# Layer 0's scores and values as 64×64 matmuls on the quadrants of the array, in turns

## The chip, the cores and the metric

The kernel runs on one core of one Trainium2 chip. A core has TensorE (PE, with its weight loads shown as PEld), VectorE (DVE), ScalarE (ACT), GpSimd (POOL) and SyncE (SP, which here issues DMAs), all with instruction queues of their own that meet through semaphores. The metric is the device time of the whole program in microseconds (us). Before the change it is 2517.85 us, the median of three runs (2517.65 to 2518.61). The profiled execution is a separate one; its span is 2627.8 us, and all times inside it are read against that span.

## The reference

Two layers work on 8 items of 1024 tokens with 256 channels. The change touches only the attention of layer 0:

```
qkv = (xt @ w_qkv + b_qkv).reshape(B, S, 8, 3 * 64)
q, k, v = jnp.split(qkv, 3, axis=-1)
attn = jnp.einsum('bihd,bjhd->bijh', q, k) * SCALE
attn = jax.nn.softmax(attn, axis=1)
res = jnp.einsum('bijh,bjhd->bihd', attn, v).reshape(B, S, 512)
res = res @ w_out + b_out + xt
```

The softmax runs over axis 1, the queries i: for one key j the exponentials over all queries are summed. So the sum belongs to a key, and the kernel divides the values of a key by it instead of the weights. Layer 1 is a single-head attention with a layer norm, then a mixture of 8 experts with 2 chosen per token. All is in f32.

## The kernel before

The items are worked one after the other: layer 0 of an item (`layer0`), its layer 1 attention (`attend`), norm and routing. The routing of an item (`gates`, `dispatch`) is a generator whose small pieces are put into the steps of the next item's layer 0. The experts follow after seven items; the eighth has its experts computed densely.

In `layer0` the 8 heads form 4 pairs g (`NPAIR`). Heads of a pair lie on partitions 0 to 63 and 64 to 127 of the q and k tiles. There are 32 steps `at`, that is 4 pairs times 8 blocks j of 128 keys. One step works one key block of both heads h:

- `score(at, h, n)` is a matmul of 64 rows (the head's channels), 128 columns (the keys) and 512 queries (half n). It writes one PSUM bank of the tile `psc`, of which the pool `ps_big` has three (two banks each, shared with the projections `pqk` and others). Head 0 uses the upper half of the array's rows, head 1 the lower, so that two of them can run side by side.
- `first_max` (DVE, line 401) takes the maximum over the first 512 queries, and `soften` (DVE, line 413) over the second, giving `nmax`. ACT then writes the exponentials `ex` with their sum (line 423), which frees the `psc` tile. After head 1, DVE takes the reciprocal of the sums (line 430) and scales the values to `vs` (line 432).
- `gather_values(at)` runs two steps later (`LAG = 2`): four matmuls of 128 rows (keys), 64 columns (channels of one head) and 512 queries, which accumulate over the 8 key blocks in the two banks `po`. After the last key block ACT copies both banks to `res` (line 457).
- In steps j = 3 and j = 5 of the first three pairs `project` computes q or k of the next pair: four full-array matmuls `pqk` (line 299), evicted by DVE (line 289).

The loop in `layer0` emits per step: score (at, 0, 0), then score (at-1, 1, 1), scores (at, 0, 1) and (at, 1, 0), then the four value matmuls. DVE's order of the maxima is pinned by `tc.issue_after`. The framework's planner settles each engine's final order and adds the semaphores; in the built program each step has four scores in a row and then four values in a row on PE.

A tile of `psc` is reused by the third allocation after it: score (at+1, 0, 0) takes the tile of (at-1, 1) and so waits for its exponential.

Of the kernel before, what the change touches and what calls it, by code (L numbers as in the profile page):

```python
# [12 lines left out]
AF = mybir.ActivationFunctionType  # L13
ALU = mybir.AluOpType
AX = mybir.AxisListType


@with_exitstack
def kernel(
# [23 lines left out]
    nc = tc.nc  # L43
    P = 128
# [3 lines left out]
    DK = 64  # L48
    SCALE = DK ** (-0.5)
    NCC = C // P  # L50
    NT = S // P
    NH2 = S // 512
# [21 lines left out]
    def big(name):  # L74

        return ps_big.tile([P, 1024], F32, tag="big", name=name)

    def acc(name):

        return ps_acc.tile([P, 512], F32, tag="acc", name=name)  # L80
# [126 lines left out]
    def bcast(t, n):  # L207

        return t.unsqueeze(2).to_broadcast([P, NT, n])
# [159 lines left out]
    def layer0(b, xT, begun, routing):  # L369

        v, qks = begun.v, begun.qks
        array = None
        res = one.tile([P, NPAIR, S], F32, tag="res", name=f"res_{b}")
        steps = [(g, j) for g in range(NPAIR) for j in range(NT)]
        LAG = 2
        seconds = {}  # L380
        pss, firsts, nmaxes, exps, sums, vss = {}, {}, {}, {}, {}, {}
        po = None

        def score(at, h, n):
            g, j = steps[at]
            q, k = qks[g]
            if n == 0:
                pss[at, h] = big(f"psc_{b}_{g}_{j}_{h}")
            r = slice(h * DK, (h + 1) * DK)
            mm = nc.tensor.matmul(  # L390
                pss[at, h][:, ts(n, 512)], k[r, ts(j, P)], q[r, ts(n, 512)], start=True, stop=True
            )
            if n == 1:

                tc.declare_no_dep(mm.ins, firsts.pop((at, h)).ins, reason="the other bank")

        def first_max(at, h):

            g, j = steps[at]
            nmax = small.tile([P, 1], F32, tag="nmax1", name=f"nmax1_{b}_{g}_{j}_{h}")  # L400
            firsts[at, h] = nc.vector.tensor_reduce(  # L401
                nmax, pss[at, h][:, ts(0, 512)], AX.X, ALU.max, negate=True
            )
            nmaxes[at, h] = nmax

        def soften(at, h):

            g, j = steps[at]
            ps = pss.pop((at, h))
            if h == 0:  # L410
                sums[at] = small.tile([P, 2], F32, tag="sums", name=f"sums_{b}_{g}_{j}")
            nmax = small.tile([P, 1], F32, tag="nmax", name=f"nmax_{b}_{g}_{j}_{h}")
            seconds[h] = nc.vector.tensor_scalar(  # L413
                scrap,
                ps[:, ts(1, 512)],
                -1.0,
                nmaxes.pop((at, h)),
                ALU.mult,
                ALU.min,
                accum_out=nmax,  # L420
            )
            ex = expp.tile([P, 1024], F32, tag="exps", name=f"ex_{b}_{g}_{j}_{h}")
            nc.scalar.activation(  # L423
                ex, ps, AF.Exp, bias=nmax, scale=1.0, accum_out=sums[at][:, h : h + 1]
            )
            exps[at, h] = ex
            if h == 1:

                rs = small.tile([P, 2], F32, tag="rs", name=f"rs_{b}_{g}_{j}")
                nc.vector.reciprocal(rs, sums.pop(at))  # L430
                vs = four.tile([P, 2, DK], F32, tag="vs", name=f"vs_{b}_{g}_{j}")
                nc.vector.tensor_mul(
                    vs,
                    v[:, j, ts(g, P)].rearrange("p (h d) -> p h d", d=DK),
                    rs.unsqueeze(2).to_broadcast([P, 2, DK]),
                )
                vss[at] = vs

        def gather_values(at):
            nonlocal po  # L440
            g, j = steps[at]
            if j == 0:
                po = [acc(f"po_{b}_{g}_{n}") for n in range(NH2)]
            vs = vss.pop(at)
            exs = [exps.pop((at, h)) for h in range(2)]
            for n in range(NH2):
                for h in range(2):
                    mm = nc.tensor.matmul(  # L448
                        po[n][h * DK : (h + 1) * DK, :],
                        vs[:, h, :],  # L450
                        exs[h][:, ts(n, 512)],
                        start=(j == 0),
                        stop=(j == NT - 1),
                    )
            if j == NT - 1:
                for n in range(NH2):
                    nc.scalar.copy(res[:, g, ts(n, 512)], po[n])
            return mm

        last = len(steps) - 1  # L460
        for at in range(last + LAG + 1):
            if at <= last:
                score(at, 0, 0)
            if 0 < at <= last + 1:
                score(at - 1, 1, 1)
                soften(at - 1, 1)
            if at <= last:

                with tc.issue_after(seconds[1].ins) if 1 in seconds else nullcontext():
                    first_max(at, 0)  # L470
                score(at, 0, 1)
                score(at, 1, 0)
                soften(at, 0)
                with tc.issue_after(seconds[0].ins):
                    first_max(at, 1)
            if at == 0:
                begun.rest()
                next(routing, None)
            if at >= LAG:
                array = gather_values(at - LAG)  # L480
            if at <= last:
                g, j = steps[at]
                if g + 1 < NPAIR and j in (3, 5):
                    if j == 3:
                        qks.append([])
                    qks[g + 1].append(project(b, xT, g + 1, len(qks[g + 1])))
                if array is not None:
                    with tc.issue_after(firsts[at, 1].ins), tc.issue_after(array.ins):
                        next(routing, None)
        for _ in routing:  # L490
            pass


        t1 = one.tile([P, NT, C], F32, tag="t1", name=f"t1_{b}")
        n = 1024 // C
        for i in range(0, NT, n):
            pt = big(f"pt_x_{b}_{i}")
            for j in range(n):
                for cc in range(NCC):
                    nc.tensor.transpose(  # L500
                        pt[:, j * C + cc * P : j * C + (cc + 1) * P], xT[:, cc, ts(i + j, P)], ident
                    )
            nc.vector.tensor_add(
                t1[:, i : i + n, :],
                pt.rearrange("p (j c) -> p j c", c=C),
                b_o.unsqueeze(1).to_broadcast([P, n, C]),
            )
        for i in range(NT):
            pr = acc(f"pr_{b}_{i}")
            for g in range(NPAIR):  # L510
                nc.tensor.matmul(  # L511
                    pr[:, :C], res[:, g, ts(i, P)], wo[:, g, :], start=(g == 0), stop=(g == NPAIR - 1)
                )
            nc.vector.tensor_add(t1[:, i, :], pr[:, :C], t1[:, i, :])
        return t1


    def attend(b, t1, fill, step=nothing):
# [22 lines left out]
        def scores(i):  # L541
# [10 lines left out]
            nmax = small.tile([P, 1], F32, tag="nmax", name=f"nmax_{b}_{i}")  # L552
            nc.vector.tensor_reduce(nmax, psc, AX.X, ALU.max, negate=True)  # L553
            ex = expp.tile([P, 1024], F32, tag="exps", name=f"ex1_{b}_{i}")
# [55 lines left out]
    def gates(b, lT):  # L610


        def tmp(tag):
            return small.tile([P, NT, E], F32, tag=tag, name=f"{tag}_{b}", bufs=1)

        def col(tag):
            return small.tile([P, NT], F32, tag=tag, name=f"{tag}_{b}", bufs=1)
# [12 lines left out]
        m = col("g_m")  # L630
        nc.vector.tensor_reduce(m, l, AX.X, ALU.max)
        p = tmp("g_p")
# [3 lines left out]
        z = col("g_z")  # L636
        nc.vector.tensor_reduce(z, p, AX.X, ALU.add)
        nc.vector.reciprocal(z, z)
# [3 lines left out]
        def first_of_max(src, tag):  # L642
            top, best = col(f"{tag}_top"), col(f"{tag}_best")
            hot = tmp(f"{tag}_hot")
            nc.vector.tensor_reduce(top, src, AX.X, ALU.max)
            nc.vector.tensor_tensor(hot, src, bcast(top, E), ALU.is_equal)
            yield
            nc.vector.tensor_mul(hot, hot, rank)
            nc.vector.tensor_reduce(best, hot, AX.X, ALU.max)
            nc.vector.tensor_tensor(hot, hot, bcast(best, E), ALU.is_equal)  # L650
# [565 lines left out]
```

## Time and profile before

| | us | share of the span or count |
|---|---|---|
| time, median of 3 | 2517.85 | |
| span of the profiled run | 2627.8 | |
| PE busy | 2504.9 | 95% |
| DVE busy | 1538.1 | 59% |
| ACT busy | 891.0 | 34% |
| POOL busy | 386.0 | 15% |
| layer 0 of one item (559 to 720 us): span 161, PE busy | 151.01 | |
| the same stretch, DVE and ACT busy | 111.04 and 80.41 | |

How to read it: busy PE time is the union of records, whose ends are modelled, so it says that PE is rarely without work and not that the array is full. An f32 matmul appears as two records (passes) and two weight loads, so 1024 score matmuls are x2048. A row of the list of groups has line, engine, operation, written and read tiles, shapes and count, then busy time, mean of one in ns, and the engine's idle time before them with what ended most of it. A row of the timeline has start, length, engine, line, operation and count; neighbouring equal instructions are merged.

### The profile page before, as it was taken

How to read it: one execution, taken by the hardware profiler on the slowest of the kernel's cores; microseconds unless marked ns; L12 is line 12 of the kernel's file. 1: busy time of each engine (PE TensorE's matmuls, PEld its weight loads, DVE VectorE, ACT ScalarE, POOL GpSimd, SP SyncE). 2: the span in 40 equal slices, each digit the busy share in tenths (PEclk: the TensorE clock that was granted, in tenths of full speed). 3: DMA queues.
4: the chain of work that ended last, by engine and by line, in shares of the span. 5: the costliest groups of instructions: out<-in, count | busy, mean ns of one | idle time of the engine just before them, and what ended most of it. 6: DMA issues, size and time to landing. Idle time of an engine off the chain costs nothing.

```text
span 2627.8 us, 27548 instructions
## 1 busy us (share of the span) xinstructions
PE 2504.9 (95%) x9919; PEld 1311.3 (50%) x9919; DVE 1538.1 (59%) x3738; ACT 891.0 (34%) x1491; POOL 386.0 (15%) x383
## 2 busy tenths in 40 slices
PE   9999989998999989998999899989998999997798
PEld 3346434643365336532563256324643488884566
DVE  5764766466656765576557664766476753334443
ACT  3541345134512542244214431444144422221212
POOL 0000020002000100002000200020002144435561
PEclk9999999999999999999999999999999999998899
DMA  7991000000000000000000000000000156663352
GB/s 289 385 333 44 32 33 17 1 17 33 1 17 17 19 15 17 16 1 33 17 17 1 32 17 0 17 32 1 0 17 33 53 196 225 214 196 100 104 166 103
DMA packets 82513, 187.61 MB, mean 71 GB/s; under 512 B 13992, under 2 KB 23880, under 8 KB 80584
## 3 DMA queue, kind: packets, MB, share of 16 engines
q1 hardware_dynamic: 57368, 118.65, 12.6%
q0 software_dynamic: 25008, 67.20, 8.2%
q8 instruction: 78, 1.28, 0.2%
q14 instruction: 59, 0.48, 0.1%
HBM read 100.49 MB, written 110.90 MB: 80 GB/s over the span
## 4 chain that ended last, share of the span: by engine, by line
PE 88%; DVE 3%; another core or an unknown queue 3%; issue 2%; DMA 2%; ACT 2%; SPq 0%; ACTq 0%; POOL 0%; DVEq 0%; POOLq 0%
PE psc L390 19%; PE po L448 17%; PE pqk L299 9%; PE py L571 8%; PE ps L545 7%; PE pr L511 4%; PE pv L335 4%; PE ph L903 3%; PE pe L928 3%; PE pdy L1110 2%; PE pdh L1086 2%; PE px L530 2%; PE pa L564 2%; PE pt_n L232 1%
## 5 line engine op out<-in xcount | busy, mean ns | idle before, releaser
L423 ACT ACTIVATE ex<-psc,nmax 128x1024 f32<-128x1024 f32 x512 | 570.5, 1114 | 639.5 <-DVE scrap L413 576.2
L390 PE MATMUL psc<-qk,qk 64*128 64x512 f32 x2048 | 553.3, 622 | 12.6 <-ACT ex L423 8.1
L413 DVE TENSOR_SCALAR_CACHE_REDUCE scrap<-psc,nmax 128x512 f32<-128x512 f32 x512 | 384.2, 750 | 229.7 <-PE psc L390 137.4
L448 PE MATMUL po<-ex,vs 128*64 128x512 f32 x2048 | 495.9, 605 | 2.1 <-DVE nmax L401 2.1
L390 PEld LDWEIGHTS psc<-qk,qk 64*128 64x128 f32 x2048 | 209.8, 185 | 337.7 <-ACT ex L423 176.1
L401 DVE TENSOR_REDUCE nmax<-psc 128x1 f32<-128x512 f32 x512 | 347.4, 679 | 16.6 <-PE psc L390 16.0
L299 PE MATMUL pqk<-xT,wqkv 128*128 128x512 f32 x512 | 249.8, 633 | 53.8 <-ACT ex L423 53.8
L448 PEld LDWEIGHTS po<-ex,vs 128*64 128x64 f32 x2048 | 124.8, 136 | 337.7 <-issue 212.5
L571 PE MATMUL py<-n,aT 128*128 128x256 f32 x1024 | 244.4, 393 | 16.7 <-DVE aT L566 11.9
L571 PEld LDWEIGHTS py<-n,aT 128*128 128x128 f32 x1024 | 196.0, 195 | 81.9 <-DVE aT L566 49.7
L545 PE MATMUL ps<-nT,xa 128*128 128x512 f32 x512 | 236.5, 592 | 0.0
L692 POOL TENSOR_TENSOR t<-t,n 128x2048 f32<-128x2048 f32 x8 | 36.3, 4537 | 1280.2 <-issue 1004.4
L299 PEld LDWEIGHTS pqk<-xT,wqkv 128*128 128x128 f32 x512 | 99.1, 201 | 195.8 <-issue 102.6
L763 POOL DMA_INDIRECT rows<-n,d_at x112 | 109.2, 975 | 593.3 <-DVE d_at L757 561.3
L556 ACT ACTIVATE ex<-ps,nmax 128x1024 f32<-128x1024 f32 x64 | 71.3, 1115 | 352.2 <-DVE nmax L553 321.9
L576 DVE SCALAR_TENSOR_TENSOR t<-py,rs,t 128x256 f32<-128x256 f32 x64 | 31.0, 484 | 232.6 <-PE py L571 201.7
L289 DVE TENSOR_SCALAR qk<-pqk,b_qk 128x512 f32<-128x512 f32 x100 | 75.1, 751 | 121.4 <-PE pqk L299 121.4
L545 PEld LDWEIGHTS ps<-nT,xa 128*128 128x128 f32 x512 | 93.6, 190 | 79.9 <-issue 73.7
L975 POOL DMA_INDIRECT yk<-y,yat x112 | 112.4, 1003 | 122.1 <-DVE o L1007 71.8
L335 PE MATMUL pv<-wqkv,xT 128*128 128x512 f32 x256 | 119.6, 596 | 1.0 <-ACT wqkv L105 1.0
L553 DVE TENSOR_REDUCE nmax<-ps 128x1 f32<-128x1024 f32 x64 | 78.3, 1224 | 59.1 <-PE ps L545 54.1
L511 PE MATMUL pr<-wo,res 128*128 128x256 f32 x512 | 111.8, 379 | 0.0
(191 smaller groups left out, 2426.9 us busy)
## 6 DMA issues: line engine op xcount, KB each, us to landing
rows<-wb SPq DMA_DIRECT2D x7, 8192.0 KB
y<-yb SPq DMA_DIRECT2D x63, 256.0 KB
xT<-in_x_dram SPq DMA_DIRECT2D x7, 1024.0 KB
sums<-t SPq DMA_DIRECT2D x7, 1024.0 KB
o<-sums SPq DMA_DIRECT2D x7, 1024.0 KB
out_dram<-oT SPq DMA_DIRECT2D x14, 512.0 KB
wpack<-in_L_ffn_w_dram SPq DMA_DIRECT2D x4, 1024.0 KB
wb<-in_L_ffn_w_dram SPq DMA_DIRECT2D x16, 256.0 KB
```

Source lines behind the costliest of these rows:

```text
L299: mm = nc.tensor.matmul(pq[:, ts(n, 512)], wqkv[:, cc, t, ts(g, P)], xT[:, cc, ts(n, 512)], start=(cc == 0), stop=(cc == NCC - 1),)
L335: nc.tensor.matmul(pv, self.xT[:, cc, ts(i, P)], wqkv[:, cc, 2, :], start=(cc == 0), stop=(cc == NCC - 1),)
L390: mm = nc.tensor.matmul(pss[at, h][:, ts(n, 512)], k[r, ts(j, P)], q[r, ts(n, 512)], start=True, stop=True)
L401: firsts[at, h] = nc.vector.tensor_reduce(nmax, pss[at, h][:, ts(0, 512)], AX.X, ALU.max, negate=True)
L413: seconds[h] = nc.vector.tensor_scalar(scrap, ps[:, ts(1, 512)], -1.0, nmaxes.pop((at, h)), ALU.mult, ALU.min, accum_out=nmax,)
L423: nc.scalar.activation(ex, ps, AF.Exp, bias=nmax, scale=1.0, accum_out=sums[at][:, h : h + 1])
L448: mm = nc.tensor.matmul(po[n][h * DK : (h + 1) * DK, :], vs[:, h, :], exs[h][:, ts(n, 512)], start=(j == 0), stop=(j == NT - 1),)
L511: nc.tensor.matmul(pr[:, :C], res[:, g, ts(i, P)], wo[:, g, :], start=(g == 0), stop=(g == NPAIR - 1))
L545: nc.tensor.matmul(psc[:, ts(n, 512)], xa[:, ec, ts(i, P)], nT[:, ec, ts(n, 512)], start=(ec == 0), stop=(ec == NCC - 1),)
L571: nc.tensor.matmul(py[:, :D], aT[:, ts(m, P)], n1[:, m, :], start=(m == 0), stop=(m == NT - 1))
L763: nc.gpsimd.indirect_dma_start(out=view[:, :], out_offset=bass.IndirectOffsetOnAxis(ap=at[:, i : i + 1], axis=0), in_=n2[:, i, :], in_offs ...
L975: nc.gpsimd.indirect_dma_start(out=yk[:, i, k, :], out_offset=None, in_=self.group.y[:, :], in_offset=bass.IndirectOffsetOnAxis(ap=ats[k][ ...
```

## The change

Scores and values are cut into matmuls of 64 rows by 64 columns, so that both kinds use the same quarter tiles of the array and no change of tiling lies between them. A score of 128 keys becomes two of 64 keys (c = 0, 1) into the two partition halves of the same bank. A value matmul over 128 keys becomes two over 64 keys each (`half`), on the upper or lower rows. Both halves must add into the same bank; so they take turns: in turn 0 the upper half works on bank 0 and the lower on bank 1, in turn 1 the reverse. `gather_values` is called twice a step, and the step becomes scores, values, scores, values.

A value group of one half must not write a bank while the other half still does. This is kept by a relay: after each half's last matmul an empty instruction (`nop`) is put on another engine (GpSimd for the first item, SyncE for the others), which waits for PE; the first matmul of the other half in the next turn waits for it.

```diff
+        relay = nc.gpsimd if b == 0 else nc.sync
...
-            mm = nc.tensor.matmul(
-                pss[at, h][:, ts(n, 512)], k[r, ts(j, P)], q[r, ts(n, 512)], start=True, stop=True
-            )
...
+            for c in range(2):
+                mm = nc.tensor.matmul(
+                    pss[at, h][ts(c, DK), ts(n, 512)],
+                    k[r, j * P + c * DK : j * P + (c + 1) * DK],
+                    q[r, ts(n, 512)],
...
-        def gather_values(at):
+        def gather_values(at, turn):
...
+            for half in range(2):
+                keys = ts(half, DK)
+                n = (half + turn) % 2
                 for h in range(2):
                     mm = nc.tensor.matmul(
-                        po[n][h * DK : (h + 1) * DK, :],
-                        vs[:, h, :],
-                        exs[h][:, ts(n, 512)],
-                        start=(j == 0),
-                        stop=(j == NT - 1),
+                        po[n][ts(h, DK), :],
+                        vss[at][keys, h, :],
+                        exps[at, h][keys, ts(n, 512)],
+                        start=(j == 0 and turn == 0),
+                        stop=(j == NT - 1 and turn == 1),
                     )
+                    if h == 0 and (j > 0 or turn > 0):
+                        tc.add_manual_dep(mm.ins, turned[1 - half].ins.name, BEHIND)
+                turned[half] = relay.nop()
+                tc.add_manual_dep(turned[half].ins, mm.ins.name, BEHIND)
...
                 soften(at - 1, 1)
+            if at >= LAG:
+                gather_values(at - LAG, 0)
             if at <= last:
...
             if at >= LAG:
-                array = gather_values(at - LAG)
+                array = gather_values(at - LAG, 1)
```

More of the change, by code (lines that the diff above doesn't have):

```diff
@@ L15 @@
 AX = mybir.AxisListType
+BEHIND = mybir.DependencyInfo(mybir.DependencyClass.Sync, mybir.DependencyReason.DATA)
 @with_exitstack
@@ L379, in layer0 @@
         LAG = 2
-        seconds = {}
+        seconds, turned = {}, {}
+        relay = nc.gpsimd if b == 0 else nc.sync
         pss, firsts, nmaxes, exps, sums, vss = {}, {}, {}, {}, {}, {}
@@ L389, in score @@
             r = slice(h * DK, (h + 1) * DK)
-            mm = nc.tensor.matmul(
-                pss[at, h][:, ts(n, 512)], k[r, ts(j, P)], q[r, ts(n, 512)], start=True, stop=True
-            )
-            if n == 1:
-                tc.declare_no_dep(mm.ins, firsts.pop((at, h)).ins, reason="the other bank")
+            for c in range(2):
[3 more added lines that the diff above has]
+                    q[r, ts(n, 512)],
+                    start=True,
+                    stop=True,
+                )
+                if n == 1:
+                    tc.declare_no_dep(mm.ins, firsts[at, h].ins, reason="the other bank")
         def first_max(at, h):
@@ L437, in soften @@
                 vss[at] = vs
-        def gather_values(at):
+        def gather_values(at, turn):
             nonlocal po
             g, j = steps[at]
-            if j == 0:
+            if j == 0 and turn == 0:
                 po = [acc(f"po_{b}_{g}_{n}") for n in range(NH2)]
-            vs = vss.pop(at)
-            exs = [exps.pop((at, h)) for h in range(2)]
-            for n in range(NH2):
+            for half in range(2):
+                keys = ts(half, DK)
+                n = (half + turn) % 2
                 for h in range(2):
                     mm = nc.tensor.matmul(
-                        po[n][h * DK : (h + 1) * DK, :],
-                        vs[:, h, :],
-                        exs[h][:, ts(n, 512)],
-                        start=(j == 0),
-                        stop=(j == NT - 1),
-                    )
+                        po[n][ts(h, DK), :],
[3 more added lines that the diff above has]
+                        stop=(j == NT - 1 and turn == 1),
+                    )
+                    if h == 0 and (j > 0 or turn > 0):
+                        tc.add_manual_dep(mm.ins, turned[1 - half].ins.name, BEHIND)
+                turned[half] = relay.nop()
+                tc.add_manual_dep(turned[half].ins, mm.ins.name, BEHIND)
+            if turn == 0:
+                return mm
+            vss.pop(at)
+            for h in range(2):
+                exps.pop((at, h))
             if j == NT - 1:
```

## The prediction

> **What bounds the kernel now.** First the shares: PE is busy 95% of the span, and the chain that ended last is 88% PE. So layer 0 has to be read from PE's own timeline. The groups of the lines concerned (busy us, mean ns, then idle time before them):
>
> ```profile
> L423 ACT ACTIVATE ex<-psc,nmax 128x1024 f32<-128x1024 f32 x512 | 570.5, 1114 | 639.5 <-DVE scrap L413 576.2
> L390 PE MATMUL psc<-qk,qk 64*128 64x512 f32 x2048 | 553.3, 622 | 12.6 <-ACT ex L423 8.1
> L413 DVE TENSOR_SCALAR_CACHE_REDUCE scrap<-psc,nmax 128x512 f32<-128x512 f32 x512 | 384.2, 750 | 229.7 <-PE psc L390 137.4
> L448 PE MATMUL po<-ex,vs 128*64 128x512 f32 x2048 | 495.9, 605 | 2.1 <-DVE nmax L401 2.1
> L401 DVE TENSOR_REDUCE nmax<-psc 128x1 f32<-128x512 f32 x512 | 347.4, 679 | 16.6 <-PE psc L390 16.0
> ```
>
> Scores and values hold PE for 1049 us, and waits before them are only 12.6 and 2.1 us. What a pass costs is seen where nothing switches, in layer 1:
>
> ```profile
> 507.61 1.88 PE L545 MATMUL ps<-nT,xa 128*128 128x512 f32 x4
> 509.32 1.04 PE L564 MATMUL pa<-ident,ex 128*128 128x128 f32 x8
> ```
>
> Four passes take 1.71 us from start to start: 0.43 each. In layer 0:
>
> ```profile
> 583.81 3.70 PE L299 MATMUL pqk<-xT,wqkv 128*128 128x512 f32 x8
> 587.44 2.04 PE L390 MATMUL psc<-qk,qk 64*128 64x512 f32 x8
> 589.40 1.94 PE L448 MATMUL po<-ex,vs 128*64 128x512 f32 x8
> 591.27 2.06 PE L390 MATMUL psc<-qk,qk 64*128 64x512 f32 x8
> ```
>
> Eight passes two at a time would be 1.71. The scores take 1.96, the values 1.87, and the projection 3.63 for 3.43. So each change of tiling costs 0.16 to 0.25 us, and a step 3.83, of which 3.42 is streaming.
>
> The other chain in a step leads from a score to the reuse of its `psc` tile:
>
> ```profile
> 670.32 0.75 DVE L413 TENSOR_SCALAR_CACHE_REDUCE scrap<-psc,nmax 128x512 f32<-128x512 f32 x1 [0.73 <-PE psc L390]
> ...
> 671.17 1.11 ACT L423 ACTIVATE ex<-psc,nmax 128x1024 f32<-128x1024 f32 x1 [1.15 <-DVE scrap L413]
> ...
> 672.19 0.19 ACT L423 ACTIVATION_READ_ACCUMULATOR ex<-psc,nmax 128x1 f32 x1
> ```
>
> The first score pair of this block, begun at 669.14, has streamed by 670.10; DVE starts 0.22 later, ACT 0.85 after that, and ACT ends 1.21 later (672.38). A weight load elsewhere (592.21) starts 0.05 after such an end (592.16). Score start to reuse is 0.86 + 0.22 + 0.85 + 1.21 + 0.05 = 3.19 us. Before, score (at-1, 1, 1) opens a step and the tile is wanted when the next opens, 3.83 later: no wait.
>
> **The Trainium skill.** "TensorEngine Tiling (Array Packing)", Tiling Modes: changing the tiling mode, not merely the tile, drains the array. The trace agrees, with 0.16 to 0.25 us. The same page, Restrictions and Gotchas: different row tiles cannot write the same PSUM bank at once; hence the relay. No run shows a breach. "TensorE: Matmul & The Clock Gate", Part 3: matmuls on disjoint tiles run side by side. The trace agrees for two (eight passes in 1.87 us); four at once it doesn't show.
>
> **Part by part.** (1) Count and streaming: score and value instructions double, each on a quarter instead of half of the array. With four at once 16 + 16 passes are again 8 slots of 0.43 = 3.42 us a step. A quarter's weight load has 64 columns, 0.14 us as on line 448, beside a slot of 0.43: free unless it waits.
>
> (2) Removed: two switches in a step without a projection, 0.41 us.
>
> (3) Relay: no row shows the empty instruction. PE to DVE takes 0.22, ACT to PE 0.05; with the smallest record (0.08) in between about 0.35, bounded by 0.27 and, if SyncE were slow, 0.86. A bank is wanted by the other half one score slot (0.86) after it is free, so one half merely lags the other: I take nothing. SyncE's few DMA issues stand ahead of its layer.
>
> (4) The order. The built program's PE queue, with names shortened, is in every ordinary step:
>
> ```
> score (at+1) head 0, first half, c0        waits for ACT
> values, lower rows, turn 1 of this step    waits for the relay
> score (at+1) head 0, first half, c1
> score (at) head 1, second half, c0 and c1
> values, upper rows, turn 0                 waits for the relay and DVE
> ```
>
> The first row waits for exponential (at-1, 1). Behind it in the in-order queue stand the lower rows' values and then score (at, 1, 1), which starts the next such chain on the same rows. The loop is therefore 0.86 for the values plus the 3.19 above: 4.05 us a step, not 3.42. DVE is reordered too: the reciprocal, which waits for that exponential, now stands ahead of the second maximum of head 0. This chain is 0.85 + 1.21 + 0.05 and then 0.08 + 0.28 + 0.75 + 0.68 of DVE, 3.9 a step, and hides beside 4.05; routing pieces on DVE (some 0.2 each) add in places. An ordinary step becomes 4.05 to 4.4, I take 4.13: +0.3 on 3.83. The step after a projection has its exponentials done and runs at 3.42: -0.4.
>
> (5) Projections. In 47 of the 48 projections the built queue isn't one block any more: 46 times it has the first `pqk` matmul, then the lower rows' values alone, then the other three; once all four are parted by values. That is two more switches (0.4) and 0.86 on half an array, whose upper rows idle (0.43 to 0.86 lost), plus entering late: +0.9 to +1.4, I take +1.15.
>
> (6) Pair ends. The last values on the lower rows now end behind the score that waits for ACT; then ACT must copy both `po` banks (0.59 each) before the new pair's values, which are only 0.86 away and hold up everything behind them. Before, a block of scores (1.96) lay between. 0.22 + 1.17 + 0.05, plus up to 1.2 of an exponential ahead on ACT: 1.4 to 2.6, less what overlaps; I take +2.0.
>
> (7) Layer ends. Steps 30 and 31 leave eight half groups of values. The built queue puts two transposes `pt_x` (line 500) between each, where before seven transposes lay between two full blocks. Eight groups alone are 8 x 0.86 against 4 x 0.86 (+3.4), and 16 switches against 4 are 12 x 0.19 (+2.3): +5.7.
>
> Sum for one item: 15 ordinary steps x 0.3 = +4.5; 6 after a projection x -0.4 = -2.4; 6 projections x 1.15 = +6.9; 3 pair ends x 2.0 = +6.0; layer end +5.7: +20.7 us. Times 8: +166. Nothing else hides it, as PE has no idle time here. 2517.85 + 166 = 2684.
>
> **The rivals.** *A, faster:* nothing waits and the split projections and ends cost little. The 3.83 in the profile and the small waits speak for it, since DVE's 3.46 busy in a step (2 x 0.75, 2 x 0.68, 0.16, 0.28 and two accumulator reads) fits beside PE. 24 steps x 8 x 0.41 = -79; one more pair of switches for each projection (48 x 0.4 = +19) and for the layer ends (8 x 1.5 = +12): 2470. Against it stands the order of the queue. *B, slower by less:* the ACT wait and the pair ends hide, for instance if lower-row work isn't held behind the waiting load, but (5) and (7) hold: -79 + 55 + 46 = +22, so 2540. *C, slow relay:* the round trip is over 0.86, say 1.2, so both turns lose 0.35: 2 x 256 x 0.35 = +180 on top, partly beside the waits of (4): 2800. Against: the hand-overs of 0.05 to 0.22.
>
> **How the numbers follow.** The forecast 0.72, A 0.10, B 0.13, C 0.05. Time: 2684. Bounds of the forecast: ordinary steps 0.2 to 0.5 (-12 to +24), projections 0.9 to 1.4 (+-12), pair ends 1.2 to 2.6 (-19 to +14), switches 0.16 to 0.25 (-4 to +7), which together reach about 2640 to 2740. The range takes in B: 2535 to 2745, leaving out A, C and slips of the forecast. Slower: the forecast, C and most of B, 0.87; within 0.2% 0.03, cut from A and B; faster 0.10.
>
> **What would show it.** `psc` and `po` at twice their counts. PE's wait of the scores for ACT, 8.1 us before, grows to 40 or more; DVE's idle time before the reciprocal (10.9 us before, all for ACT) grows past 80. In PE's timeline, ordinary steps repeat every 4.05 to 4.4 us, a gap of 1 to 3 us stands before the first `po` of a pair with ACT's copy as its releaser, `pqk` splits in x2 and x6, and `po` x4 alternates with `pt_x` x2 at the end. Layer 0 of an item grows from 161 us to some 182. I am wrong if steps run at 3.4 to 3.6 (no blocking), if four quarters don't stream at once (a step near 6.8), or if waits for SP or POOL lead PE's list.

## The result, and the profile after

The changed kernel takes 2833.17 us (2832.85 to 2834.29, four runs) beside 2518.17 us of the kernel before on the same chip: 1.125 times as long, interval 1.123 to 1.127. The direction was forecast, the size was not: 315 us more, where the forecast had 166 and its range ended at 2745.

The groups of the lines concerned, from the page of the changed kernel (busy us, mean ns, then idle time before them and its main releaser):

```profile
L459 PE MATMUL po<-ex,vs 64*64 64x512 f32 x4096 | 1083.5, 612 | 8.2 <-ACT res L478 7.5
L395 PE MATMUL psc<-qk,qk 64*64 64x512 f32 x4096 | 1040.4, 599 | 6.8 <-ACT ex L432 6.6
L432 ACT ACTIVATE ex<-psc,nmax 128x1024 f32<-128x1024 f32 x512 | 570.1, 1113 | 832.0 <-DVE scrap L422 809.5
L439 DVE RECIPROCAL rs<-sums 128x2 f32<-128x2 f32 x256 | 42.3, 165 | 183.3 <-ACT ex L432 183.2
```

Twice the count of matmuls was planned. Busy time has doubled as well: with four quarters working at once it should have stayed near 553 and 496. And yet PE waits for nearly nothing: 8.2 and 6.8 us. Each of the two kinds is "busy" with one or two quarters at a time: 4096 passes of 0.43 us are 1761 us of streaming, so in 1083.5 busy us only 1.6 value passes ran at once. The timeline shows how this comes about; here is one step of PE (start, length, engine, line, operation, count):

```profile
430.13 0.65 PE L459 MATMUL po<-ex,vs 64*64 64x512 f32 x2
430.29 0.60 PE L395 MATMUL psc<-qk,qk 64*64 64x512 f32 x2
430.61 0.60 PE L459 MATMUL po<-ex,vs 64*64 64x512 f32 x2
431.04 0.59 PE L395 MATMUL psc<-qk,qk 64*64 64x512 f32 x1
431.31 0.65 PE L459 MATMUL po<-ex,vs 64*64 64x512 f32 x2
431.32 0.74 PE L395 MATMUL psc<-qk,qk 64*64 64x512 f32 x2
431.79 0.59 PE L459 MATMUL po<-ex,vs 64*64 64x512 f32 x2
431.80 1.01 PE L395 MATMUL psc<-qk,qk 64*64 64x512 f32 x3
432.58 0.65 PE L459 MATMUL po<-ex,vs 64*64 64x512 f32 x2
```

Read the `po` rows alone. Two rows x2 are one half group: the first passes of both heads, 0.48 later their second passes. The groups begin at 430.13, 431.31 and 432.58, and then at 433.75 and 434.93: one every 1.2 us, never two together. A step has four of them, and 4 x 1.2 is the step: ACT's exponentials of head 0 are 4.79 us apart in ordinary steps, where they were 3.83. Between the last passes of a group (431.79) and the first of the next (432.58) lie 0.79 us, of which 0.43 is streaming: the relay's hand-over, from PE to the other engine and back, takes 0.36 us there, and some 0.26 us before the other three groups of a step.

Who stands in between shows in the waits of SyncE's queue (us in all, times, longest):

```profile
SPq L469 <- PE po L459: 1116.5, 683, 12.7
```

Line 469 is the relay's empty instruction. That SyncE waits for PE is its task; that PE waits for it is hardly listed anywhere, since the half groups on the other rows and the scores keep some part of PE at work.

**Why one after the other.** The code says it, and the text ahead of the prediction read it wrongly. `turned[half]` is set inside the loop over the halves. When half 1 of a turn is emitted, `turned[1 - half]` is already the relay of half 0 of the *same* turn, not of the turn before. So half 1 of a turn waits for half 0 of it, and half 0 for half 1 of the turn before: a single chain through every half group of a pair, although the two halves of one turn write different banks.

The end of a layer shows that chain bare (PE's timeline):

```profile
519.50 1.08 PE L459 MATMUL po<-ex,vs 64*64 64x512 f32 x4
520.51 0.44 PE L523 MATMUL pt_x<-ident,xT 128*128 128x128 f32 x2
520.88 1.08 PE L459 MATMUL po<-ex,vs 64*64 64x512 f32 x4
521.88 0.44 PE L523 MATMUL pt_x<-ident,xT 128*128 128x128 f32 x2
```

Eight groups, each with two transposes of 0.37 in its hand-over, follow one another at 1.37 us.

Item 0 gives the account of the whole. (The profiled execution of the kernel before has stalls of 8 to 16 us in each later item, and its span is 110 us longer than its timed runs; item 0 is free of them. So the 161 us of a layer shown ahead of the prediction are too many: it is about 147.) The steps are ACT's starts of head 0's exponentials:

| item 0, us | before | after | difference | forecast |
|---|---|---|---|---|
| first 3 and 10 ordinary steps | 52.57 | 63.93 | +11.4 | +4.5 (15 steps) |
| 6 steps with a projection | 44.97 | 52.10 | +7.1 | +6.9 |
| 6 steps after one | 23.01 | 31.57 | +8.6 | -2.4 |
| 6 steps round pair ends | 22.90 | 29.92 | +7.0 | +6.0 (3 ends) |
| last exponential to layer 1's first score | 34.1 | 39.4 | +5.3 | +5.7 |
| sum | 177.6 | 216.9 | +39.4 | +20.7 |

39.4 x 8 = 315 us, as measured. (The items differ a little, and it evens out: items 2 to 6 have 175.9 us where item 0 has 177.5, item 1 has 187.9.) But for the first three steps every kind of step has grown by 1.0 to 1.4 us: a cost of every step, not of special ones.

### The profile page after: what moved, and what is told of

It is laid out like the page before. It is cut to its first block, busy times and chain, and to the rows that moved or that the text cites. A ratio compares the mean times of both kernels' runs of the same rounds, so it can differ in the third digit from the quotient of the medians.

```text
span 2831.1 us, 36680 instructions
## 1 busy us (share of the span) xinstructions
PE 2780.1 (98%) x14015; PEld 1426.0 (50%) x14015; DVE 1571.1 (55%) x3738; ACT 889.5 (31%) x1491; POOL 386.2 (14%) x383
## 4 chain that ended last, share of the span: by engine, by line
PE 78%; DVE 3%; ACT 3%; DMA 2%; issue 1%; ACTq 0%; POOL 0%; SPq 0%; POOLq 0%; DVEq 0%
PE po L459 21%; PE psc L395 14%; PE pqk L300 7%; PE py L594 7%; PE ps L568 6%; PE pr L534 3%; PE ph L926 3%; PE pe L951 3%; PE pv L336 3%; ACT ex L432 2%; PE pdy L1133 2%; PE pdh L1109 2%; PE px L553 2%; PE pa L587 2%; DVE scrap L422 1%; PE pt_n L233 1%
## 5 line engine op out<-in xcount | busy, mean ns | idle before, releaser
L459 PE MATMUL po<-ex,vs 64*64 64x512 f32 x4096 | 1083.5, 612 | 8.2 <-ACT res L478 7.5
L395 PE MATMUL psc<-qk,qk 64*64 64x512 f32 x4096 | 1040.4, 599 | 6.8 <-ACT ex L432 6.6
L395 PEld LDWEIGHTS psc<-qk,qk 64*64 64x64 f32 x4096 | 330.2, 133 | 541.4 <-issue 471.7
L459 PEld LDWEIGHTS po<-ex,vs 64*64 64x64 f32 x4096 | 210.5, 131 | 249.8 <-issue 87.6
L594 PE MATMUL py<-n,aT 128*128 128x256 f32 x1024 | 238.3, 386 | 4.8 <-DVE aT L589 4.8
L300 PEld LDWEIGHTS pqk<-xT,wqkv 128*128 128x128 f32 x512 | 89.4, 189 | 148.7 <-issue 109.1
L439 DVE RECIPROCAL rs<-sums 128x2 f32<-128x2 f32 x256 | 42.3, 165 | 183.3 <-ACT ex L432 183.2
```

Source lines behind the costliest of these rows:

```text
L300: mm = nc.tensor.matmul(pq[:, ts(n, 512)], wqkv[:, cc, t, ts(g, P)], xT[:, cc, ts(n, 512)], start=(cc == 0), stop=(cc == NCC - 1),)
L395: mm = nc.tensor.matmul(pss[at, h][ts(c, DK), ts(n, 512)], k[r, j * P + c * DK : j * P + (c + 1) * DK], q[r, ts(n, 512)], start=True, stop ...
L459: mm = nc.tensor.matmul(po[n][ts(h, DK), :], vss[at][keys, h, :], exps[at, h][keys, ts(n, 512)], start=(j == 0 and turn == 0), stop=(j == ...
L594: nc.tensor.matmul(py[:, :D], aT[:, ts(m, P)], n1[:, m, :], start=(m == 0), stop=(m == NT - 1))
```

## The experiments

The kernel before took 2515 us beside these runs. Theory S is the serial chain of half groups; theory D is the loop of DVE and ACT that step 4 of the forecast described (the reciprocal stands ahead of the second maximum on DVE). First four kernels that touch the relay and the split.

**The relay on the turn before** (e1_prev_turn). The marks in `turned` are copied when a turn begins, and the copy is read:

```diff
+            was = dict(turned)
...
-                        tc.add_manual_dep(mm.ins, turned[1 - half].ins.name, BEHIND)
+                        tc.add_manual_dep(mm.ins, was[1 - half].ins.name, BEHIND)
```

> Each half group of values waits for the other half's group of the turn before, not of the same turn (a copy of the marks is taken at the start of the turn). Theory S (serial): in the changed kernel the four half groups of a step follow one another, each waiting for the relay of the one just before it, 4 x 1.2 = 4.8 us a step; here two run at once and a relay has 0.86 us to arrive, so an ordinary step is 3.42 to 3.6 us and 24 such steps x 8 items save 0.25 to 0.41 against 3.83: 2440 to 2470 us in all. Rival R1 (the relay is slow in itself): its waits stay in every turn, at or above 2700. Rival R2 (quarter tiles don't stream four at once): about 2830 as with the change.

Measured 2620.13 us (2617.21 to 2622.72), ratio 1.042 [1.040, 1.044]. One index takes away 213 of the 315 us: S is the larger part of the loss, but the gain that S alone promised doesn't come, which was a miss. The busy time of both kinds falls by a third, since more quarters now work at once:

```profile
L460 PE MATMUL po<-ex,vs 64*64 64x512 f32 x4096 | 717.8, 607 | 51.0 <-ACT res L479 43.0
L395 PE MATMUL psc<-qk,qk 64*64 64x512 f32 x4096 | 724.8, 614 | 11.6 <-ACT ex L432 10.5
```

The built queue changes with the edit, so the run alone can't part the two: no projection is parted any more, in ordinary steps the two half groups of a turn stand in one block where the changed kernel has scores in between, and layer 1 starts 35.0 us after the last exponential, not 39.4. That the waiting and not the order carries the loss is read from the 0.26 to 0.36 us between the groups, and tested by the second hop below.

**No relay at all** (e2_own_bank). Each half has a bank of its own in both turns, so the kernel leaves out the correct sums.

```diff
-                        po[n][ts(h, DK), :],
+                        po[half][ts(h, DK), :],
...
-                    if h == 0 and (j > 0 or turn > 0):
-                        tc.add_manual_dep(mm.ins, turned[1 - half].ins.name, BEHIND)
-                turned[half] = relay.nop()
-                tc.add_manual_dep(turned[half].ins, mm.ins.name, BEHIND)
```

> No relay at all: each half writes a bank of its own in both turns, so nothing is shared (the two query halves are then added up in the wrong bank; instructions, shapes and streams stay the same). S: the relay of the turn before is hidden in the kernel with copied marks, so this one is within 10 us of it, 2430 to 2470. R1: faster than that one by 60 or more. R2: about 2830.

Measured 2608.32 us, ratio 1.037 [1.035, 1.038]. The relay as such costs 12 us over the whole program once it has the right turn to wait for, and 10.7 of them lie in item 1 (162.9 us of layer 0 for 152.2), the first with its relay on SyncE: there the built queue holds values back behind scores and a projection, and in e1_prev_turn none starts from 307 to 318 us. So the forecast's reason for step 3 (one half lags the other by a slot, which hides a hand-over) is right for the relay it described; the kernel has another one. And 93 us stay that no relay explains.

**Scores in quarters, values as before** (e3_scores_only).

```diff
+            for c in range(2):
                 mm = nc.tensor.matmul(
-                    pss[at, h][:, ts(n, 512)], k[r, ts(j, P)], q[r, ts(n, 512)], start=True, stop=True
+                    pss[at, h][ts(c, DK), ts(n, 512)],
+                    k[r, j * P + c * DK : j * P + (c + 1) * DK],
```

> Only the scores are cut into quarter tiles; the values stay 128 rows by 64 columns, in one block a step, without relay. S and the switch theory: two switches of tiling remain in each step, four quarters stream at once, so 2518 within 15 us. R2: a score block takes up to twice its 1.71 us, so up to +1.7 x 256 = +440, 2950.

Measured 2508.03 us, ratio 0.997 [0.996, 0.998]. PE's timeline of this kernel:

```profile
420.55 2.04 PE L391 MATMUL psc<-qk,qk 64*64 64x512 f32 x16
422.52 1.94 PE L453 MATMUL po<-ex,vs 128*64 128x512 f32 x8
424.39 1.99 PE L391 MATMUL psc<-qk,qk 64*64 64x512 f32 x16
```

Sixteen passes take 1.97 us, as eight did before: four quarters do stream at once, and neither the split nor its doubled weight loads cost anything.

**A second hop in the relay** (e4_two_hops), the other engine's empty instruction behind the first:

```diff
-                turned[half] = relay.nop()
-                tc.add_manual_dep(turned[half].ins, mm.ins.name, BEHIND)
+                hop = relay.nop()
+                tc.add_manual_dep(hop.ins, mm.ins.name, BEHIND)
+                turned[half] = (nc.sync if b == 0 else nc.gpsimd).nop()
+                tc.add_manual_dep(turned[half].ins, hop.ins.name, BEHIND)
```

> The changed kernel with two empty instructions in series, on SyncE and GpSimd, for each hand-over. S: every half group is on the path, four a step; a hand-over longer by 0.06 to 0.2 us and some 900 half groups outside the projections give +50 to +180 us on 2833: 2885 to 3010. If the order of PE's queue or the tile size were the cause and the relay hidden (R2 and the forecast): 2833 within 15 us.

Measured 3062.27 us, ratio 1.217 [1.215, 1.219]: 229 us more than the changed kernel. Three parts make it up. In items 1 to 7 the ordinary step goes from 4.79 to 4.99 us, four hand-overs longer by 0.05 each, and layer 0 from 175.9 to 181.3 in items 2 to 6; together these seven layers grow by 32 us (item 1 has lost the stall it had). The layer ends grow by 2.2 each, 18 in all. These 50 us are the lower end of what S was given. The rest was not expected: in item 0 a single step lasts 175.31 us, and the layer grows by 180. There SyncE is in the relay, behind its DMA issues. The values wait for line 471, the second empty instruction, and the chain that ended last names one of the issues, line 246:

```profile
L459 PE MATMUL po<-ex,vs 64*64 64x512 f32 x4096 | 1089.6, 614 | 171.6 <-SPq L471 161.9
```

```profile
PE po L459 24%; PE psc L395 14%; PE pqk L300 8%; PE py L596 7%; PE ps L570 6%; SPq L246 4%; PE pr L536 4%; PE pv L336 3%; PE ph L928 3%; PE pe L953 3%; ACT ex L432 2%; PE pdy L1135 2%; PE px L555 2%; PE pa L589 2%; PE pdh L1111 2%; DVE scrap L422 2%
```

Four per cent of 3061 us is 122. The relay of item 0 on GpSimd keeps clear of that queue. And a chain in which 0.05 us in a hand-over comes back four times in every step is one in which every half group lies on the path: S again.

What is left in the kernel with the mended relay (105 us, or 93 without a relay) shows on its DVE (timeline, the bracket is the idle time before and its releaser):

```profile
430.81 0.17 DVE L439 RECIPROCAL rs<-sums 128x2 f32<-128x2 f32 x1 [0.73 <-ACT ex L432]
431.01 0.29 DVE L441 TENSOR_TENSOR vs<-v,rs 128x128 f32<-128x128 f32 x1
431.22 0.75 DVE L422 TENSOR_SCALAR_CACHE_REDUCE scrap<-psc,nmax 128x512 f32<-128x512 f32 x1
...
434.79 0.17 DVE L439 RECIPROCAL rs<-sums 128x2 f32<-128x2 f32 x1 [0.73 <-ACT ex L432]
```

The reciprocal waits 0.73 us for an exponential, the second maximum waits behind it in the queue, the next exponential waits for that maximum: 3.98 us a round, where step 4 had worked out 3.9. Three kernels ask about this loop and about the pair ends.

**The reciprocal and the product where they were before** (e5_divide_later), behind the second maximum:

```diff
-            if h == 1:
-                rs = small.tile([P, 2], F32, tag="rs", name=f"rs_{b}_{g}_{j}")
...
+        def divide(at):
...
                 soften(at, 0)
+                if at > 0:
+                    with tc.issue_after(seconds[0].ins):
+                        divide(at - 1)
                 with tc.issue_after(seconds[0].ins):
                     first_max(at, 1)
```

> The kernel of e1_prev_turn (relay on the turn before), with the reciprocal of step at-1 and its product with the values put on DVE behind the second maximum of head 0 of step at, where the kernel before has them, instead of ahead of it. Theory D (what is left after the relay is the chain in which DVE's reciprocal waits for the exponential and the second maximum, and so the next exponential, waits behind it): ordinary steps fall from 3.97 us to 3.43 to 3.6; 15 of them an item x 8 x about 0.45 = 54 us, and the longer steps with routing pieces (4.4 to 4.7) fall too, 20 to 60 us more: 2500 to 2550. It would fall below the kernel before only if the projections gained as well. Rival T (what is left lies in pair ends, split tiling and layer ends, and the DVE order hides beside PE): within 15 us of 2620.

Measured 2509.60 us (2506.60 to 2512.67), ratio 0.998 [0.997, 0.999]. PE's order is the same to the last row as in the kernel with the mended relay; only DVE's differs. So D is shown: 110 us for the place of two small instructions, and the kernel is now just ahead of the kernel before. Ordinary steps are 3.66 us. Not all of the 110 is the loop itself. With the mended relay alone PE waits 1.7 to 1.9 us at each of the 24 pair ends, and within 2 us of the end of 15 of these waits begins a stretch of 3.4 us in which the trace shows a granted TensorE clock of 0.5; with one more such stretch elsewhere in layer 0 they can cost up to 27 us. Here the waits are 0.9 us, and only one such stretch is left in layer 0. The mean granted clock of the timed runs agrees: 0.984 there, 0.994 here. The shares of the chain that ended last move as they should. The kernel with the mended relay:

```profile
PE 62%; DVE 14%; ACT 8%; issue 2%; DMA 2%; ACTq 0%; DVEq 0%; SPq 0%; POOLq 0%
```

This one:

```profile
PE 78%; DVE 6%; ACT 2%; issue 1%; DMA 1%; ACTq 0%; SPq 0%; DVEq 0%; POOLq 0%
```

**One of the two copies at a pair's end on DVE** besides (e6_one_copy_dve):

```diff
-                for n in range(NH2):
-                    nc.scalar.copy(res[:, g, ts(n, 512)], po[n])
+                nc.vector.tensor_copy(res[:, g, ts(0, 512)], po[0])
+                nc.scalar.copy(res[:, g, ts(1, 512)], po[1])
```

> As e5_divide_later, and of the two copies of the finished value banks at a pair's end (0.59 us each on ACT) one is made by DVE, so that both can run at once. If pair ends wait for ACT's two copies in a row (step 6 of the forecast, +2.0 each), 24 ends inside the layers x 0.6 to 1.2 = 14 to 29 us less than e5_divide_later. If the ends wait for something else, or DVE is as late as ACT, within 8 us of it.

Measured 2504.77 us, ratio 0.995 [0.994, 0.997]: 5 us less, not 14 to 29. PE still waits 0.9 us at each of the 24 ends, as in the kernel without this edit (21.2 us there in 24 waits):

```profile
PE po L462 <- ACT res L481: 21.0, 24, 0.9
```

The timeline shows why: DVE copies its bank from 927.73, but ACT's copy stands behind an exponential begun at 927.04 and starts at 928.15. (A copy ahead of that exponential wasn't tried.) In the kernel with the mended relay but the late maxima the same line read 43.0 us in 24 waits, 1.8 each: step 6's +2.0, which the serial chain hides in the changed kernel (7.5 us) and the late product halves.

**The kernel before with the changed kernel's DVE order** (e7_before_divide_first), and nothing else:

```diff
-            seconds[h] = nc.vector.tensor_scalar(
+            with tc.issue_after(divided[0].ins) if h == 0 and divided else nullcontext():
+                seconds[h] = nc.vector.tensor_scalar(
...
-                nc.vector.tensor_mul(
+                divided[0] = nc.vector.tensor_mul(
```

> The kernel before, in halves of the array, with one thing of the changed kernel: the reciprocal of step at-1 and its product stand ahead of the second maximum of head 0 of step at on DVE. Theory D (DVE and ACT then form a loop of 0.85 + 1.21 + 0.05 + 0.08 + 0.28 + 0.75 + 0.68 = 3.9 us, longer than a step of 3.83): ordinary steps go from 3.83 to 3.95 to 4.1, and those with routing pieces to 4.4 or more: 18 x 8 x 0.15 = 20 us to 60 us more, 2535 to 2575. Rival T (the order on DVE hides beside PE's own work): within 8 us of 2516.

Measured 2640.07 us, ratio 1.050 [1.048, 1.052]: 125 us, twice the upper end of what D was given. The loop itself fits, with steps of 3.98. What was left out is that, outside the steps with routing pieces, every second step is 4.73. PE has its four scores in one block; when a score in it has waited for its exponential, the block takes 3.00 us instead of 1.96 (107.21 to 110.21), and its scores come late to DVE too. That the loop then leads through PE is a reading of the timeline; no run isolates it. In item 0, steps with a projection go from 7.5 to 8.2 on average, and the 31 steps from 143.4 to 159.2 us, which times 8 is 126, the whole of it. DVE's timeline of a step of 4.73:

```profile
110.62 0.17 DVE L431 RECIPROCAL rs<-sums 128x2 f32<-128x2 f32 x1 [0.73 <-ACT ex L424]
...
113.26 0.75 DVE L414 TENSOR_SCALAR_CACHE_REDUCE scrap<-psc,nmax 128x512 f32<-128x512 f32 x1 [0.87 <-PE psc L390]
...
115.35 0.17 DVE L431 RECIPROCAL rs<-sums 128x2 f32<-128x2 f32 x1 [0.73 <-ACT ex L424]
```

Beside the 0.73 for ACT stands another 0.87 for PE: from reciprocal to reciprocal 4.73 us.

Two causes, then, and the last three kernels ask how they go together, what a parted projection costs, and what the idea can give.

**The changed kernel with the DVE order alone mended** (e8_serial_divide_later; relay as it is, the edit of e5_divide_later):

> The changed kernel with its relay as it is (within the turn), and the reciprocal with its product behind the second maximum of head 0, as in e5_divide_later. It completes the square of two causes: both 2833, relay alone mended 2620, both mended 2510, and here the DVE order alone mended. If the slower of two loops sets the step (relay 4.79 us, DVE and ACT 3.97 us), mending the shorter one changes nothing: steps stay at 4.79, within 20 us of 2833. If the two add up, it gives what it gave in e5_divide_later, 110 us: 2723.

Measured 2810.50 us (2810.43 to 2810.74), ratio 1.117 [1.115, 1.119].

| us | DVE order of the changed kernel | DVE order of before |
|---|---|---|
| relay within the turn | 2833.17 (ordinary step 4.79) | 2810.50 (4.79) |
| relay on the turn before | 2620.13 (3.98) | 2509.60 (3.66) |

The longer of two loops sets the step. In each row PE's order is the same and DVE's alone differs. That gives 23 us beneath the serial relay, a little more than was expected, and 110 without it. The gain lies at pair ends, where two steps take 9.08 us instead of 9.95, and in the first steps of a layer; ordinary steps stay at 4.79, and steps after a projection gain the 0.4 that steps with one lose.

**Projections kept whole** (e10_whole_projection), in the changed kernel:

```diff
-                    qks[g + 1].append(project(b, xT, g + 1, len(qks[g + 1])))
+                    with tc.issue_after(array.ins):
+                        qks[g + 1].append(project(b, xT, g + 1, len(qks[g + 1])))
```

> The changed kernel with the four matmuls of each projection held behind the values of the turn, so that no values stand between them on PE's queue; relay and DVE order stay. Step 5 of the forecast (a parted projection costs two switches and 0.86 on half an array, 0.9 to 1.4): 48 x 0.9 to 1.4 = 43 to 67 us less, 2766 to 2790. Rival: in a serial relay the parting costs little, as the half groups run one by one anyway and the first matmul fills the time of a hand-over; within 15 us of 2833, or slower.

Measured 2832.48 us, ratio 1.126 [1.124, 1.128]. No gain: a projection of two and six passes round a half group costs no more than one of eight. In items 2 to 6 the whole projections even make a layer 1.1 us longer (177.0 for 175.9), and a shorter stall in item 1 (182.2 for 187.9) evens it out. The parting that step 5 saw in the queue is real, and free here (timeline of the changed kernel):

```profile
417.29 1.12 PE L300 MATMUL pqk<-xT,wqkv 128*128 128x512 f32 x2
418.35 1.07 PE L459 MATMUL po<-ex,vs 64*64 64x512 f32 x4
419.35 2.84 PE L300 MATMUL pqk<-xT,wqkv 128*128 128x512 f32 x6
```

The first two passes stand where values would have waited for a hand-over.

**The scaled values ahead of the next maximum** (e9_scaled_first). In e5_divide_later and e6_one_copy_dve the step is 3.66 us, since DVE puts a maximum of 0.6 between the reciprocal and the product, for which the values wait. On top of e6_one_copy_dve:

```diff
-                with tc.issue_after(seconds[0].ins):
+                with tc.issue_after(divided[0].ins if at > 0 else seconds[0].ins):
                     first_max(at, 1)
```

> As e6_one_copy_dve, and the product of the values with the reciprocal stands ahead of the first maximum of head 1 on DVE (in e5 and e6 it runs behind it). Theory: what keeps their step at 3.66 us is the loop second maximum (0.67), first maximum of head 1 (0.59 until the product starts), product (0.28), values, scores, second maximum; taking the 0.6 of the maximum out of it leaves the 3.42 of streaming or a little more. Steps of 3.42 to 3.5: 0.16 to 0.24 x some 20 steps x 8 = 26 to 38 us less than e6_one_copy_dve, 2467 to 2479. Rival: the maximum, now later, delays the next exponential by as much, steps stay at 3.6 or more, within 10 us of 2505.

Measured 2484.62 us (2482.29 to 2487.27), ratio 0.988 [0.986, 0.989], 20 us less than e6_one_copy_dve and 30 less than the kernel before. Ordinary steps are 3.43 us, and PE's timeline is what the change was made for:

```profile
420.88 1.04 PE L462 MATMUL po<-ex,vs 64*64 64x512 f32 x8
421.74 1.04 PE L395 MATMUL psc<-qk,qk 64*64 64x512 f32 x8
422.60 1.04 PE L462 MATMUL po<-ex,vs 64*64 64x512 f32 x8
423.46 1.04 PE L395 MATMUL psc<-qk,qk 64*64 64x512 f32 x8
```

Eight passes every 0.86 us, four at a time, with nothing between. The gain is some 6 us below what was expected, as steps with routing pieces on DVE stay at 3.8 to 4.05 and pair ends at 4.57.

## Why the prediction was wrong

**Step 3 failed.** It took "nothing" for the relay, because "a bank is wanted by the other half one score slot (0.86) after it is free". The size of a hand-over was right: about 0.35 forecast, 0.26 to 0.36 measured. What waits for it was wrong: the hand-over sits between the two halves of one turn too. So a step is 4 x (0.48 + 0.43 + about 0.29) = 4.8 us and not 3.42. The way to it was in the ten lines of the diff: a mark written in the loop that reads it. The rival with a slow relay came near in time (2800), but by a hand-over of 1.2 us that no run shows.

**The wait that the forecast built on is there, and hidden.** Steps of 4.05 to 4.4, with PE's scores waiting for ACT, were forecast from two loops in step 4. The PE loop of 4.05 shows nowhere: scores wait 6.6 us for ACT, not 40. Whether it would bind is not shown: the queue that it was worked out from exists only beneath the serial relay, and with the mended relay the planner puts both halves' values behind whole scores. The DVE loop of 3.9 is real (3.98 in the kernel with the mended relay, where mending it gave 110 us), but beneath 4.79 it is worth 23 us. The wait of the reciprocal for ACT, forecast past 80 us, is 183.

**After a projection** a step was to run at 3.42. It takes 5.26, as the chain of values doesn't care that exponentials are done: with +8.6 in place of -2.4 us an item this line is the furthest off of the sum, by 11.0; the ordinary steps are off by 6.9, for the same reason.

**Projections and pair ends** have sums that fit (7.1 for 6.9, 7.0 for 6.0), by accident: they too contain the +1.0 of every step. Parting the projections costs nothing that could be measured. The pair end's wait for ACT's copies is 1.8 us without the serial chain, as forecast, and 0.3 with it.

**Layer ends** came out as forecast, 5.3 for 5.7. The queue with two `pt_x` between the groups was read rightly; but with the mended relay it is 0.9, so this cost belongs to step 3 too, by the waiting or by the order in which the queue was then built.

**Steps 1 and 2 were right:** quarters stream four at a time, and a step without waits or changes of tiling is 3.43 us, 0.40 less than the 3.83 before, for 0.41 forecast.

Two of the signs named would have misled. A layer was forecast at 182 us and shows 181, but from a true start of about 147, not 161. And "waits for SP lead PE's list" doesn't happen (8.2 us before `po` in all), though SyncE's relay sets the time.

The gain of the last kernel can be told from its layers. They take 135.6 us in item 0, 137.9 to 138.3 in items 2 to 6, 144.5 in item 1, where values are held back as told above, and 144.1 in item 7. For the kernel before, 143.4 is known from item 0; taking it for every item, with 3.4 more in item 7 as in e3_scores_only, the eight layers gain 36 us, and less 0.9 at each layer end 29; 30 were measured. What stays open is the PE loop of 4.05, and why the clock of 0.5 follows some pair-end waits and not others.

## What to carry to other kernels

When a change adds a wait by hand, write out for two rounds which instruction waits for which mark, at the moment the mark is read: whether a mark is copied before or overwritten in the loop decides between a lag of one slot and a single chain. A busy engine with no waits is no proof of an engine at work: compare its busy time with the count times the price of one, and look at how many run at once. And when two loops are near each other, mend both before judging the idea: either mended alone still lost to the kernel before, both together came out just ahead of it, and with one product moved 30 us ahead.

## What the hardware showed besides

A hand-over from PE through an empty instruction on SyncE and back took 0.26 to 0.36 us from the end of streaming to the next matmul; through GpSimd in item 0 the step is 4.85 instead of 4.79, 0.015 us more for each; a second hop adds only 0.05. Four f32 matmuls of 64 x 64 on the four quarters stream together at 0.43 us a pass, as one on the whole array does. Two instructions of 0.16 and 0.28 us on an engine that is 59% busy cost 125 us by their place in the queue alone.
